# Four transformer layers on one core: image 1 loaded behind all weights, experts of image 0 with every fourth group of tangents, eight buffers for combined outputs

## The chip, the cores and the metric

The kernel runs on one core of a Trainium2 chip. The metric is the device time of one execution in microseconds (us). Its engines work side by side, each through its own list of instructions in order: PE (TensorE, matrix products and the transposes made with an identity matrix), DVE (VectorE), ACT (ScalarE), POOL (GpSimd) and SP (SyncE), which issues most of the DMAs. ACT issues some DMAs too, from the same list that holds its activations, and POOL issues the gathers and scatters. An instruction that has to wait holds up everything behind it on its engine. In the profile, "SPq" and "ACTq" are the DMA issues of SP and ACT.

## What is computed

Two images of 256 channels and 32x32 pixels (1024 tokens each, N) go through four layers. Cut to what matters:

```python
x = x + conv_attention(group_norm(x))        # layer 0: 4 heads of 64, every token of both images attends to all
x = linear_attention_block(x)                # layer 1: per image, 8 heads of 64, softmax attention, residual
t = tokens(x)
t = t + window_attention(layer_norm(t))      # layer 2: windows of 64
t = t + moe(layer_norm(t))                   # layer 2: 8 experts, top 2, 256 -> 1024 -> 256, gelu
# layer 3: additive attention, per image
q, k = u @ Wt, u @ Wx                        # u = layer_norm(t), 32 units
e = (tanh(q[:, None] + k[None] + bh) @ Wa)   # 1024 x 1024 x 32 tangents per image
t = t + softmax(e) @ u
t = t + moe3(layer_norm(t))                  # layer 3: 8 experts, top 2, 256 -> 512 -> 256, gelu
out = pixels(t)
```

Only the two chosen experts of each token are computed. The tokens are sorted by expert on the chip into blocks of 128 rows; a block is gathered, multiplied with its expert's weights, and scattered to a buffer in DRAM, from which each token's two results are read back and added with their router weights.

## The kernel before

**Front (layers 0 and 1).** `run` loads image 0 (`image(xT, 0)`, lines 1370 to 1375: per 128 channels one large DMA on SP and a small one on ACT, since the pixels are stored turned by 32). `front` (line 336) then loads Wk, Wq, Wv and the biases on SP, then image 1, then calls `project0` (line 504) for the projections of layer 0. The weights of layers 1 and 2 (`weights()`) and Wo come after it in the program. In `project0`, each image's group norm is taken (`group_norm` L583 and L584, `pool_stats` L599 to L604, `rsqrt` L131 to L138), then the image is normalised on DVE, 1024 columns per instruction (L545), and four chunks of 512 columns are multiplied on PE into k, q and v (L529, L565). DVE and ACT take them out of PSUM. A scheduler orders each engine's instructions by its own estimate of when they can run: it put image 1's statistics (L583) between image 0's `rsqrt` steps.

**Attention of layers 0 and 1 (`attention`, line 190).** One long list of steps: chunks of 512 queries for a pair of heads, each chunk of 32 steps (layer 0) or 8 (layer 1). A step is two score products (L215, L216) on PE, an exponential on ACT (L218), a running sum on DVE (L227) and the value products (L237) on PE. What belongs to the end of a chunk is put into later steps: `divide` (L251 to L264) two steps after the chunk's last, and the chunk's `finish` four steps after (L277). For every second chunk of layer 0, `finish` is `output0` (L367, L372): the product of the divided result `q` with Wo, added to the image.

**Experts (`experts`, line 1070).** Per block: gather the rows (POOL, L1098), fetch both weight matrices (SP, L1092 and L1104), transpose the rows (PE, L1110), first product (L1127), copy (DVE, L1132), transpose (L1138), gelu with bias (ACT, L1143: four instructions of 128 columns), second product (L1151), bias (DVE, L1157), scatter (POOL, L1158). The function yields after each part of 512 hidden columns, and its callers decide between what these steps are put. A block of layer 2 has two such parts, one of layer 3 has one. Layer 2 has 39 blocks for both images together, with two buffers for weights; layer 3 has 23 per image, with three.

**Combining (`combine`, line 1188).** For each tile of 128 tokens two DMAs read the tokens' two results into a tile `yt` (one on each of two given queues), and two DVE instructions (L1197) add them to `t`. `yt` has three buffers.

**From layer 2 to layer 3 in `run`.** After 49 steps of layer 2's experts, `prepare(0)` combines image 0's eight tiles (loads on SP and on ACT), takes the statistics, normalises (L131 to L186) and projects to the keys and queries of the additive attention (L1246, L1251, L1256). Expert steps go on from its ninth step. Then the additive attention runs over 128 groups of tangents (64 per image): DVE adds the query to the keys (L1280), ACT takes the tangents (L1290, 128x4096), PE sums them with the weights (L1299); every eight groups there is a softmax (ACT L1352) and its product with the values (PE L1312, L1320). In the first half, every second group is followed by an expert step of layer 2. Around the middle, the rest of layer 2 is finished and image 1 is prepared. Then image 0 is routed for layer 3, and its experts (`first`, `third(0)`) are stepped with every third group, until the tangents end. After the tangents, the routing of image 1 (`ready(1, 1)`) alternates with steps of `first`; what is left of `first` is drained; then image 1's 23 blocks run (`third(1)`), with one step of `end(0)` each. `end` (line 1533) combines a tile, and after every fourth tile transposes two halves (L1544), copies them on ACT to `y_f` (L1549, two buffers) and stores them (L1552, L1554, both SP). At the very end `end(1)` runs alone.

The expert activation gelu and the softmax's exponential are in different tables of ACT; tangents run with either.

Of the kernel before, what the change touches and what calls it, by code (L numbers as in the profile page):

```python
# [87 lines left out]
class Stack:  # L88
# [101 lines left out]
    def attention(self, chunks, pools):  # L190

        nc = self.nc
        p_t, p_o, p_r, sb = pools
        steps = [(c, j) for c in chunks for j in range(c["n"])]
        weights = {}
        inverses = sb.tile([P, CH], F32, name="inverses", bufs=1)
        nc.gpsimd.memset(inverses, 0.0)

        def score(n):
            c, j = steps[n]  # L210
            q, (ka, kb) = c["q"](), c["k"](j)
            ps = p_t.tile([P, 2, CH], F32, name="ps_t")
            for half in range(2):
                part = slice(64 * half, 64 * half + 64)
                nc.tensor.matmul(ps[part, 0, :], lhsT=ka[:, part], rhs=q[0:64, :], start=True, stop=True)  # L215
                nc.tensor.matmul(ps[part, 1, :], lhsT=kb[:, part], rhs=q[64:128, :], start=True, stop=True)  # L216
            e = sb.tile([P, 2, CH], F32, name="e", bufs=4)
            nc.scalar.activation(e, ps, AF.Exp)  # L218
            weights[n] = e
            if j == 0:  # L220
                c["sum"] = e
            elif j == 1:
                s = sb.tile([P, 2, CH], F32, name="sum", bufs=2)
                nc.vector.tensor_tensor(s, c["sum"], e, ALU.add)
                c["sum"] = s
            else:
                nc.vector.tensor_tensor(c["sum"], c["sum"], e, ALU.add)  # L227

        def accumulate(n):
            c, j = steps[n]  # L230
            if j == 0:
                c["po"] = p_o.tile([P, 2, CH], F32, name="ps_o")
            e = weights.pop(n)
            for r, v in enumerate(c["v"](j)):
                for half in range(2):
                    part = slice(64 * half, 64 * half + 64)
                    nc.tensor.matmul(  # L237
                        c["po"][64 * r : 64 * r + 64, half, :], lhsT=v[part, :], rhs=e[part, r, :],
                        start=(j == 0), stop=(j == c["n"] - 1),
                    )  # L240
            if j == c["n"] - 1:
                o = sb.tile([P, 2, CH], F32, name="o", bufs=2)
                nc.scalar.copy(o[:, 0, :], c["po"][:, 0, :])
                nc.vector.tensor_copy(o[:, 1, :], c["po"][:, 1, :])  # L244
                c["po"] = o

        def divide(c):

            ps = p_r.tile([P, CH], F32, name="ps_row")
            for r in range(2):  # L250
                nc.tensor.matmul(  # L251
                    ps[64 * r : 64 * r + 64, :], lhsT=self.ones[:, 0:64], rhs=c["sum"][:, r, :],
                    start=True, stop=True,
                )
            total = sb.tile([P, CH], F32, name="total", bufs=1)
            number = c["number"]
            nc.scalar.activation(total, ps, AF.Copy, accum_out=self.added[:, number : number + 1])
            o = c["po"]
            nc.vector.tensor_tensor(o[:, 0, :], o[:, 0, :], o[:, 1, :], ALU.add)
            den = sb.tile([P, CH], F32, name="den", bufs=2)  # L260
            to = c["o"]()
            for half in (slice(0, CH // 2), slice(CH // 2, CH)):
                nc.vector.reciprocal(den[:, half], total[:, half])  # L263
                nc.vector.tensor_tensor(to[:, half], o[:, 0, half], den[:, half], ALU.mult)  # L264
            nc.gpsimd.tensor_tensor(inverses, inverses, den, ALU.add)  # L265


        todo = {}
        later = lambda at, *fs: todo.setdefault(at, []).extend(fs)
        at = 0  # L270
        for i, c in enumerate(chunks):
            c["at"] = at
            at += c["n"]
            c["number"] = i

            later(at + 2, lambda c=c: divide(c))
            later(at + 4, c["finish"])  # L277
            for k, extras in c.get("extras", {}).items():
                later(c["at"] + k, *extras)
            if i + 1 < len(chunks):  # L280
                later(at - 4, chunks[i + 1]["prepare"])

        chunks[0]["prepare"]()
        scored = 0
        for n in range(at + 5):
            ahead = 2 if 0 < n < at and steps[n][1] == 0 else 1
            while scored < min(n + ahead + 1, at):
                score(scored)
                scored += 1
            if n < at:  # L290
                accumulate(n)
            for f in todo.pop(n, []):
                f()
        nc.vector.tensor_reduce(self.extremes[:, 1:2], inverses, AX.X, ALU.max)
# [38 lines left out]
    def front(self, xT, weights, tokens, done):  # L333
# [6 lines left out]
        with ExitStack() as ctx:  # L340
# [3 lines left out]
            wk, wq, wv = (self.load(w, n, "(c p) o -> p c o", p=P) for n in ("wk", "wq", "wv"))  # L344
            bk, bq = (self.load(w, n) for n in ("bk", "bq"))
            bv = self.load_row(w, "bv")
            self.image(xT, 1)
            q0 = big.tile([P, CC, T], F32, name="q")
            k0 = big.tile([P, 4, T], F32, name="k")
            v0 = big.tile([P, NT, 4, 64], F32, name="v")  # L350
            with ExitStack() as start:
# [1 line left out]
                    pool(start, "l0_xn"), pool(start, "l0_ps", bufs=4, space=PSUM), xT,  # L353
                    (wq, wk, wv, bq, bk, bv), (q0, k0, v0),
                )
            w_in, w_out, gn_w, gn_b, b_out = weights()
            wo, bo = self.load(w, "wo", "(c p) o -> p c o", p=P), self.load(w, "bo")

            pools = self.attention_pools(ctx)
            p_r = pools[2]  # L360
# [13 lines left out]
            def chunk0(t, o):  # L374
                def finish():
                    if o == CC - 1:
                        output0(t)
                    if (t, o) == (NCH - 1, CC - 1):
                        first.close()
                        tokens()  # L380
                        pools1.append(pool(ctx, "l1_late", side="right"))


                cols = slice(t * CH, (t + 1) * CH)
                return {
                    "prepare": lambda: None,
                    "n": 4 * NT,
                    "q": lambda: q0[:, o, cols],
                    "k": lambda j: [
                        k0[64 * r : 64 * r + 64, j // NT, (j % NT) * P : (j % NT + 1) * P] for r in range(2)  # L390
                    ],
                    "v": lambda j: [v0[:, j % NT, j // NT, :]] * 2,
                    "o": lambda: q0[:, o, cols],
                    "finish": finish,
                }

# [111 lines left out]
    def project0(self, pool, psum, xT, weights, to):  # L508
# [26 lines left out]
        for t in range(NCH):  # L535
            cols = slice(t * CH, (t + 1) * CH)
            if t % 2 == 0:
# [2 lines left out]
                    pool, psum, xT, b,  # L540
                    lambda ps, rows: nc.tensor.matmul(ps, lhsT=group, rhs=rows, start=True, stop=True),
                )
                for c in range(CC):
                    at = slice(b * N, (b + 1) * N)
                    nc.vector.tensor_scalar(  # L545
                        xn[:, c, at], xT[:, c, at], mean[:, c : c + 1], rs[:, c : c + 1], ALU.subtract, ALU.mult
                    )


            for o in range(CC):  # L550
# [634 lines left out]
                    fetch_second(b + ahead)  # L1185
            yield True

    def combine(self, sb, t, given, top, i, queues):

        nc = self.nc  # L1190
        n = top.shape[2]
        y = sb.tile([P, 2, C], F32, name="yt", bufs=3)
        for k in range(2):
            at = (k * n + i) * P
            queues[k].dma_start(out=y[:, k, :], in_=given[at : at + P, :])
# [181 lines left out]
    def run(self):  # L1377
        tc, nc, ins = self.tc, self.nc, self.ins
        PER = N // P
        with ExitStack() as ctx:  # L1380
# [137 lines left out]

                return mixture(1, wp, lambda _: rows[1][b], given[0][b], BLOCKS, lambda _: slots)

            def prepare(b, bank, *queues):

                for i in range(b * PER, (b + 1) * PER):
                    self.combine(sb, t[:, i], all_given[b * 2 * N : (b + 1) * 2 * N], top[0][b], i - b * PER, queues)
                    stats(2, i)
                    yield
                for g in range(2 * b, 2 * b + 2):
# [2 lines left out]
                    self.additive_project(aa, g, uT, bank)  # L1530
                    yield

            def end(b, bank):

                for i in range(PER):
                    self.combine(sb, t[:, b * PER + i], given[0][b], top[1][b], i, (nc.sync, nc.scalar))
                    yield
                    if i % 4 != 3:
                        continue
# [1 line left out]
                    for c in range(CC):  # L1541
                        ps = bank()
                        for k in range(4):
# [1 line left out]
                                ps[:, k * P : (k + 1) * P], t[:, b * PER + i - 3 + k, c * P : (c + 1) * P],  # L1545
                                self.ident,
                            )
                        y = sb.tile([P, CH], F32, name="y_f")
                        nc.scalar.copy(y, ps)  # L1549
                        to = self.out[b, c * P : (c + 1) * P, :]  # L1550
                        n = min(CH, N - SHIFT - at)
                        nc.sync.dma_start(out=to[:, at + SHIFT : at + SHIFT + n], in_=y[:, :n])  # L1552
                        if n < CH:
                            nc.sync.dma_start(out=to[:, : CH - n], in_=y[:, n:])  # L1554

            with ExitStack() as side:
# [10 lines left out]
                for k in range(2 * BLOCKS + 3):  # L1569
# [4 lines left out]
                        self.extreme(other.value[4][:, 0, 0:1])  # L1574
                        inv.close()
                    second.step()
                for k, _ in enumerate(prepare(0, bank, nc.sync, nc.scalar)):
                    if k >= PER:
                        second.step()

# [2 lines left out]
            with ExitStack() as ad:  # L1583
                half = PER * self.FOURS
                bank = banks["h"]
                then = Steps(prepare(1, bank, nc.sync, nc.sync))
                routed = Steps(ready(1, 0, bank))
                first = None
                for n in self.additive_attention(
# [14 lines left out]
                    elif routed.done:  # L1604
                        if first is None:
                            first = Steps(third(0, routed.value))
                        if n % 3 == 0:
                            first.step()
            with ExitStack() as side:
                bank = in_turn(enter(side, "side_ps2", space=PSUM), "m", 3)  # L1610
# [2 lines left out]
                    other.step()  # L1613
                    first.step()
                first.drain()
                ending = Steps(end(0, bank))
                for _ in third(1, other.value):
                    ending.step()
                ending.drain()
                drain(end(1, bank))  # L1620
            weights.close()


# [556 lines left out]
```

## Time and profile before

| | us |
|---|---|
| runs (median of 3; lowest to highest) | 2527.17; 2526.05 to 2531.06 |
| the profiled execution, its own time | 2528.73 |
| its span, first to last instruction | 2527.0 |
| PE busy in the span | 2358.8 (93%) |
| DVE busy | 1703.0 (67%) |
| ACT busy | 1440.2 (57%) |
| start until the first attention score | 0 to 68.7 |
| attention of layers 0 and 1 | 68.7 to about 1330 |
| window attention and layer 2's experts alone | about 1330 to 1720 |
| combining and preparing image 0 | 1721 to 1760 |
| tangents | 1760 to 2331 |
| routing of image 1 | 2336 to 2392 |
| experts of image 1 | 2392 to 2500 |
| last combination and output | 2500 to 2527 |

Busy shares are averages over stages with different limits, so each stage has to be read by itself: a table of busy time by stretch shows which engine is full there, and the list of waits shows what the fullest engine waits for. A line of the timeline holds the start, the duration from the first start to the last end of the merged instructions, the engine, the line, and in square brackets the idle time before it with what ended it.

### The profile page before, as it was taken

The page shows a single profiled execution, that of the slowest core. Times are in us where ns is not written, and L with a number is a line of the kernel's source. Part 1 is how long each engine was busy: PE and PEld are TensorE (multiplying, and loading weights), DVE is VectorE, ACT ScalarE, POOL GpSimd, SP SyncE. Part 2 cuts the span into 40 slices and gives each one's busy share as a digit, 9 for nine tenths or more (in the row PEclk, how much of TensorE's full clock was granted, in tenths as well). Part 3 has the DMA queues.
Part 4 walks back from the last instruction along what each step waited for, and adds up shares of the span by engine and source line. Part 5 has one row for each costly group of instructions (what it writes and reads, how often), then busy time and mean ns, then how long its engine had stood idle before and what let it go on. Part 6 is the DMA issues. An engine that isn't in the chain of part 4 may idle for free.

```text
span 2527.0 us, 42429 instructions
## 1 busy us (share of the span) xinstructions
PE 2358.8 (93%) x17211; PEld 1029.1 (41%) x17211; DVE 1703.0 (67%) x2612; ACT 1440.2 (57%) x1628; POOL 240.3 (10%) x254
## 2 busy tenths in 40 slices
PE   6999999999999999999998979998999888999896
PEld 3333333333333333333333646664444333344564
DVE  4677777775677777866678566226777787786533
ACT  1565556645565566544453433222999998999221
POOL 0000000000000000000001312221110001121241
PEclk9999999999999999999999979999999999999898
DMA  4000000000000000000000037875333202233796
GB/s 133 5 1 1 1 1 2 1 1 1 1 1 1 1 2 1 1 1 1 1 1 10 2 118 265 302 284 194 138 137 136 75 9 78 86 119 115 244 337 204
DMA packets 58929, 190.51 MB, mean 75 GB/s; under 512 B 14116, under 2 KB 28964, under 8 KB 48740
## 3 DMA queue, kind: packets, MB, share of 16 engines
q1 hardware_dynamic: 45812, 161.93, 18.5%
q0 software_dynamic: 8160, 22.29, 2.4%
q10 hardware_dynamic: 4752, 3.48, 0.5%
q8 instruction: 137, 2.24, 0.4%
q14 instruction: 68, 0.56, 0.1%
HBM read 168.15 MB, written 17.43 MB: 73 GB/s over the span
## 4 chain that ended last, share of the span: by engine, by line
PE 73%; DVE 11%; issue 7%; ACT 4%; DMA 3%; POOL 1%; ACTq 0%; SPq 0%; DVEq 0%; POOLq 0%
PE ps_o L237 20%; PE ps_t L215 19%; PE ps_e L1299 8%; PE bk_h L1127 5%; PE bk_y L1151 4%; PE ps_pt L1320 2%; PE ps_row L445 2%; DVE sum L227 2%; DVE th L1280 2%; DMA w<-in_l_w 2%; ACT th L1290 1%; DVE den L263 1%; PE ps_qk L529 1%; PE ps_row L431 1%; PE bk_t L1138 1%
## 5 line engine op out<-in xcount | busy, mean ns | idle before, releaser
L227 DVE TENSOR_TENSOR sum<-sum,e 128x1024 f32<-128x1024 f32 x592 | 725.1, 1225 | 311.0 <-ACT e L218 300.9
L218 ACT ACTIVATE e<-ps_t 128x1024 f32<-128x1024 f32 x640 | 653.9, 1025 | 466.8 <-PE ps_t L216 463.5
L237 PE MATMUL ps_o<-e,v 64*64 64x512 f32 x5120 | 675.0, 591 | 8.3 <-DVE o L244 7.7
L215 PE MATMUL ps_t<-q,k 64*64 64x512 f32 x2048 | 532.3, 591 | 0.5 <-DVE v L569 0.5
L216 PE MATMUL ps_t<-q,k 64*64 64x512 f32 x2048 | 532.3, 591 | 0.0
L1280 DVE TENSOR_SCALAR th<-kT,qb 128x1024 f32<-128x1024 f32 x478 | 331.3, 750 | 95.1 <-PE ps_e L1299 92.9
L237 PEld LDWEIGHTS ps_o<-e,v 64*64 64x64 f32 x5120 | 193.8, 132 | 369.3 <-issue 178.3
L1290 ACT ACTIVATE th<-th 128x4096 f32<-128x4096 f32 x94 | 336.5, 3646 | 6.0 <-DVE th L1280 5.9
L1143 ACT ACTIVATE h<-bk_t,w 128x128 f32<-128x128 f32 x496 | 142.3, 375 | 270.4 <-issue 159.4
L1299 PE MATMUL ps_e<-th,pick 128*32 128x512 f32 x2048 | 271.8, 620 | 23.9 <-ACT p L1352 9.3
L215 PEld LDWEIGHTS ps_t<-q,k 64*64 64x64 f32 x2048 | 149.1, 133 | 287.1 <-issue 152.9
L1127 PE MATMUL bk_h<-w,xgT 128*128 128x512 f32 x496 | 245.7, 611 | 12.8 <-DVE xgT L1115 7.9
L1151 PE MATMUL bk_y<-w,h 128*128 128x256 f32 x992 | 248.3, 386 | 6.2 <-DVE y L1157 3.4
L1151 PEld LDWEIGHTS bk_y<-w,h 128*128 128x128 f32 x992 | 178.5, 192 | 56.7 <-issue 27.4
L1132 DVE COPY hp<-bk_h 128x512 f32<-128x512 f32 x124 | 85.4, 689 | 131.6 <-PE bk_h L1127 130.1
L265 POOL TENSOR_TENSOR inverses<-inverses,den 128x512 f32<-128x512 f32 x24 | 30.5, 1269 | 1333.5 <-DVE den L263 1333.5
L216 PEld LDWEIGHTS ps_t<-q,k 64*64 64x64 f32 x2048 | 149.1, 133 | 0.0
L215 PE MATMUL ps_t<-qh,kh 64*64 64x512 f32 x512 | 138.2, 597 | 0.0
L216 PE MATMUL ps_t<-qh,kh 64*64 64x512 f32 x512 | 137.3, 596 | 0.0
L1299 PEld LDWEIGHTS ps_e<-th,pick 128*32 128x32 f32 x2048 | 58.8, 111 | 170.8 <-issue 116.3
L1158 POOL DMA_INDIRECT given<-y,gives x85 | 86.9, 1022 | 415.7 <-DVE y L1157 365.2
L1127 PEld LDWEIGHTS bk_h<-w,xgT 128*128 128x128 f32 x496 | 87.4, 194 | 85.1 <-issue 56.5
(334 smaller groups left out, 2063.7 us busy)
## 6 DMA issues: line engine op xcount, KB each, us to landing
w<-in_l_w SPq DMA_DIRECT2D x39, 1152.0 KB
w<-in_l_w SPq DMA_DIRECT2D x39, 1030.0 KB
w<-in_l_w SPq DMA_DIRECT2D x46, 640.0 KB
w<-in_l_w SPq DMA_DIRECT2D x46, 514.0 KB
yt<-given SPq DMA_DIRECT2D x40, 128.0 KB
rows<-u SPq DMA_DIRECT2D x8, 512.0 KB
yt<-given ACTq DMA_DIRECT2D x24, 128.0 KB
k<-k SPq DMA_DIRECT2D x16, 128.0 KB
```

The costliest lines, as they stand in the source:

```text
L215: nc.tensor.matmul(ps[part, 0, :], lhsT=ka[:, part], rhs=q[0:64, :], start=True, stop=True)
L216: nc.tensor.matmul(ps[part, 1, :], lhsT=kb[:, part], rhs=q[64:128, :], start=True, stop=True)
L218: nc.scalar.activation(e, ps, AF.Exp)
L227: nc.vector.tensor_tensor(c["sum"], c["sum"], e, ALU.add)
L237: nc.tensor.matmul(c["po"][64 * r : 64 * r + 64, half, :], lhsT=v[part, :], rhs=e[part, r, :], start=(j == 0), stop=(j == c["n"] - 1),)
L1127: nc.tensor.matmul(ps, lhsT=inputs[b][:, c, :], rhs=first[b][:, at : at + CH], start=(c == 0), stop=(c == CC - 1),)
L1143: nc.scalar.activation(hidden[b, n][:, cols], ps[:, cols], AF.Gelu, bias=first[b][:, at : at + 1])
L1151: nc.tensor.matmul(sums[b], lhsT=h[:, j * P : (j + 1) * P], rhs=second[b][:, at : at + C], start=(n == 0 and j == 0), stop=(n == HH - 1 an ...
L1158: nc.gpsimd.indirect_dma_start(out=given[b], out_offset=index(slots(b)[1], b), in_=y, in_offset=None)
L1280: nc.vector.tensor_scalar(h[:, j, :], *keys_and_queries(n, j), None, ALU.add)
L1290: nc.scalar.activation(h, h, AF.Tanh)
L1299: nc.tensor.matmul(scored[i][U * j : U * (j + 1), a, :], lhsT=aa["pick"][:, m, :], rhs=h[:, j, a * CH : (a + 1) * CH], start=(m == 0), sto ...
```

## The change

Seven edits, in five places.

1. In `front`, all weights (of layers 1 and 2, and Wo) are loaded before image 1, which now comes last on SP's list.
2. In `project0`, the normalisation is made in pieces of 512 columns, both channel halves of the first piece ahead of the second.
3. A chunk can set its own lag; the chunks of layer 0 set it to 6, so `output0` comes six steps after the chunk's last, not four.
4. `combine` takes its pool and the number of its buffers. `prepare(0)` and both calls of `end` use a pool of their own with eight `yt` buffers; `prepare(1)` keeps three.
5. `first`, the experts of layer 3 for image 0, is stepped with every fourth group of tangents, not every third.
6. `y_f` gets four buffers, from the new pool.
7. The small second store of an output (32 columns) is issued by ACT, not by SP.

```diff
-            later(at + 4, c["finish"])
+            later(at + c.get("lag", 4), c["finish"])
...
             bv = self.load_row(w, "bv")
+            w_in, w_out, gn_w, gn_b, b_out = weights()
+            wo, bo = self.load(w, "wo", "(c p) o -> p c o", p=P), self.load(w, "bo")
             self.image(xT, 1)
...
-            w_in, w_out, gn_w, gn_b, b_out = weights()
-            wo, bo = self.load(w, "wo", "(c p) o -> p c o", p=P), self.load(w, "bo")
...
                     "o": lambda: q0[:, o, cols],
+                    "lag": 6,
                     "finish": finish,
...
-                for c in range(CC):
-                    at = slice(b * N, (b + 1) * N)
-                    nc.vector.tensor_scalar(
-                        xn[:, c, at], xT[:, c, at], mean[:, c : c + 1], rs[:, c : c + 1], ALU.subtract, ALU.mult
-                    )
+                for at in range(b * N, (b + 1) * N, CH):
+                    for c in range(CC):
+                        nc.vector.tensor_scalar(
+                            xn[:, c, at : at + CH], xT[:, c, at : at + CH],
+                            mean[:, c : c + 1], rs[:, c : c + 1], ALU.subtract, ALU.mult,
+                        )
...
-    def combine(self, sb, t, given, top, i, queues):
+    def combine(self, sb, t, given, top, i, queues, bufs=3):
...
-        y = sb.tile([P, 2, C], F32, name="yt", bufs=3)
+        y = sb.tile([P, 2, C], F32, name="yt", bufs=bufs)
...
-            def prepare(b, bank, *queues):
+            def prepare(b, bank, of, bufs, *queues):
...
-            def end(b, bank):
+            def end(b, bank, of):
...
-                    self.combine(sb, t[:, b * PER + i], given[0][b], top[1][b], i, (nc.sync, nc.scalar))
+                    self.combine(of, t[:, b * PER + i], given[0][b], top[1][b], i, (nc.sync, nc.scalar), PER)
...
-                        y = sb.tile([P, CH], F32, name="y_f")
+                        y = of.tile([P, CH], F32, name="y_f", bufs=4)
...
-                            nc.sync.dma_start(out=to[:, : CH - n], in_=y[:, n:])
+                            nc.scalar.dma_start(out=to[:, : CH - n], in_=y[:, n:])
...
-                for k, _ in enumerate(prepare(0, bank, nc.sync, nc.scalar)):
+                for k, _ in enumerate(prepare(0, bank, enter(side, "outputs2"), PER, nc.sync, nc.scalar)):
...
-                then = Steps(prepare(1, bank, nc.sync, nc.sync))
+                then = Steps(prepare(1, bank, sb, 3, nc.sync, nc.sync))
...
-                        if n % 3 == 0:
+                        if n % 4 == 0:
                             first.step()
...
-                ending = Steps(end(0, bank))
+                of = enter(side, "outputs3")
+                ending = Steps(end(0, bank, of))
...
-                drain(end(1, bank))
+                drain(end(1, bank, of))
```

More of the change, by code (lines that the diff above doesn't have):

```diff
@@ L1519, in third @@
                 return mixture(1, wp, lambda _: rows[1][b], given[0][b], BLOCKS, lambda _: slots)
-            def prepare(b, bank, *queues):
+            def prepare(b, bank, of, bufs, *queues):
                 for i in range(b * PER, (b + 1) * PER):
-                    self.combine(sb, t[:, i], all_given[b * 2 * N : (b + 1) * 2 * N], top[0][b], i - b * PER, queues)
+                    self.combine(of, t[:, i], all_given[b * 2 * N : (b + 1) * 2 * N], top[0][b], i - b * PER, queues, bufs)
                     stats(2, i)
```

## The prediction

> **What bounds the kernel now.** The page's busy shares (PE 93%) hide the stages, so the first view is busy time by stretch, with the mean clock granted to PE, the share of DMA and GB/s behind it:
>
> ```profile
> core 0: us, PE busy (x) PEld busy (x) DVE busy (x) ACT busy (x) POOL busy (x), PEclk, DMA share, GB/s
> ...
> 18.00:69.00 51.00, 45.70 (x136) 25.98 (x138) 23.02 (x52) 5.47 (x8) 0.00 (x0) 0.97 0.27 68
> 1720.00:1760.00 40.00, 31.95 (x109) 18.98 (x108) 29.18 (x94) 7.01 (x23) 4.16 (x4) 0.87 0.60 205
> ...
> 1795.00:1980.00 185.00, 181.86 (x1096) 87.77 (x1097) 144.88 (x242) 181.30 (x141) 16.42 (x15) 1.00 0.38 132
> ...
> 2155.00:2335.00 180.00, 166.57 (x1018) 75.02 (x1020) 136.54 (x239) 177.29 (x122) 29.90 (x26) 0.96 0.32 108
> 2335.00:2384.00 49.00, 44.89 (x226) 30.00 (x218) 32.26 (x116) 16.26 (x42) 11.74 (x12) 1.00 0.70 234
> 2384.00:2400.00 16.00, 7.86 (x21) 4.11 (x22) 5.08 (x15) 0.36 (x2) 6.69 (x7) 0.58 0.74 265
> ```
>
> While tangents run (1760 to 2331) ACT is full: 98% of both long stretches. PE is as full in the first half (181.86 of 185) and has room in the second (166.57 of 180). After them PE leads (44.89 of 49), then stands half idle in 2384 to 2400, the gap between the routing of image 1 and its experts. The chain of waits leads through the same places. Next, the waits of PE within the attention of layers 0 and 1:
>
> ```profile
> PE ps_row L367 <- DVE q L264: 5.1, 4, 1.3
> ```
>
> Four `output0` products of layer 0 wait 5.1 us together. Then the timeline of the ends; first the start, where image 0's normalisation (L545) waits:
>
> ```profile
> 12.28 0.70 DVE L583 BATCH_NORM_STATS2 gn_st<-xT 128x6 f32<-128x512 f32 x1 [2.02 <-DMA xT<-in_x]
> ...
> 16.42 1.54 DVE L545 TENSOR_SCALAR xn<-xT,gs,rs 128x1024 f32<-128x1024 f32 x2
> 17.29 0.50 PEld L529 LDWEIGHTS ps_qk<-xn,sb_wk 128*128 128x128 f32 x2 [7.79 <-DVE xn L545]
> ```
>
> DVE stands idle for image 1, whose statistics are in its list in the middle of image 0's `rsqrt`. Then `prepare(0)`, ACT's list:
>
> ```profile
> 1729.03 3.98 ACTq L1195 DMA_DIRECT2D yt<-given  x3
> 1736.37 1.15 ACT L1143 ACTIVATE h<-bk_t,w 128x128 f32<-128x128 f32 x4 [8.81 <-DMA yt<-given]
> ...
> 1759.88 3.62 ACT L1290 ACTIVATE th<-th 128x4096 f32<-128x4096 f32 x1 [1.01 <-DVE th L1280]
> ```
>
> ACT's gelu stands behind loads that wait for one of three `yt` buffers; PE, which needs the gelu, idles about 8 us in 1720 to 1742. Last, the gap at 2391 and the end:
>
> ```profile
> 2391.62 0.66 PE L1110 MATMUL bk_x<-ident,xg 128*128 128x128 f32 x2 [8.03 <-DMA xg<-rows,takes]
> ...
> 2393.28 3.62 PE L1127 MATMUL bk_h<-w,xgT 128*128 128x512 f32 x4
> ...
> 2502.92 7.52 ACTq L1195 DMA_DIRECT2D yt<-given  x7
> ...
> 2516.06 1.01 DVE L1197 SCALAR_TENSOR_TENSOR t<-yt,top,t 128x256 f32<-128x256 f32 x2 [1.94 <-DMA yt<-given]
> ```
>
> PE waits 8 us for gathered rows and then runs at half clock (3.62 where the same four take 1.88 elsewhere); at the end, loads are issued only as `yt` buffers come free.
>
> **What the Trainium skill says.** "DMA: Bandwidth & Descriptors", section "Issuing engines are not separate DMA queues": transfers of SP, ACT and POOL run on the same 16 engines, and a second issuer saves only the issuing time. So eight buffers let loads start, but don't widen the path; before shows both issuers held 7.5 us by buffers, not by width (125 GB/s in 2500 to 2527). "ScalarE: Activation LUTs", "What ACT_TABLE_LOAD costs": 1283 ns and a drain of some 1380 ns for every switch; the trace has 1.28 us, and its next activation starts 1.29 after, so I count no drain. "TensorE: Matmul & The Clock Gate", "What's actually happening": half clock after an idle window of about 3.4 us; 0.58 in 2384 to 2400 agrees.
>
> **The change part by part.** The sum is against the profiled execution's own 2528.73 (span 2527.0), 1.56 above the median of 2527.17.
>
> *Start.* Image 1's four statistics (4 x 0.69) and the wait leave the way: in the changed kernel's lists they come after the first v products. `rsqrt` then runs through: image 0 started it (L131) at 9.82, and for the second image L131 at 42.19 leads to L545 at 44.63, 2.44. So L545 starts at 12.26. A piece of 512 columns: 0.81 at 1024, and 0.41 at 256 in the same form (L160), so some 0.54. Products then start 0.06 later (0.87 less 0.81): 12.86 against 17.29, -4.4. For the second image the piece saves 0.27 again. PE is full between (45.70 of 51), so both reach the end: **-4.7**. Image 1 now lands behind about 6.5 MB; at some 290 to 390 GB/s that is 17 to 23 us, and DVE needs it at about 26 (the t=0 products take PE until then). If later, DVE stalls and part returns: bounds -5 and +1.
>
> *Lag.* The four `output0` go two steps back, behind score products that PE can do; two steps are longer than the 1.3 of the longest wait. Each `norm` that follows keeps about 2 us. **-5.1**, bounds -3.5 (some of it returns as waits at later products) and -5.5.
>
> *prepare(0).* All 16 loads go out together; DVE's combination (10.2 us from 1723.87) runs without pauses, and ACT is free for gelu. But SP's weight fetches now stand behind eight loads, and DVE does the whole combination ahead of the experts' copies. In the lists, 51 gelu halves stand before the first tangents, not 53. I take the normalised tokens at PE at 1738.1 instead of 1741.2, and first tangents at about 1756.9: -3.0; but two halves more (2 x 1.0 of ACT) fall into the ACT-bound tangents: +2.0. **-1.0**, bounds +5 (weights late behind the loads) and -5 (the 8 us of idle PE all filled).
>
> *Every fourth group.* Up to the last softmax ACT has 89 gelu halves, not 93, and two table loads fewer. One is 1.01 as ACT spends it: -(4 x 1.01 + 2 x 1.28) = -6.6, all in the second half, where ACT has no room and PE does. What remains of `first` grows from 8 blocks to 12. A layer 3 block is 1.72 + 0.44 + 1.73 + 0.22 = 4.1 on PE. By the lists ten of twelve run before the routing's last product, two after. So two more come beside the routing, +8.2, of which the idle there (49 - 44.89 = 4.1) can be filled and PE's lag at the last tangents (5.05) shrinks, about -5 of it in all (taken as 5.2): +3.0. Two more fall into the 8.03 wait for rows; two down products stand in PE's list behind the first gathered rows, +3.5, against a warm clock at 2393 (3.62 - 1.88): +1.8, which I take as paid for by the shorter wait ahead of it. So +3.0 for the stage, and **-3.6** in all. Bounds: +4 (nothing fills) and -9 (all fills).
>
> *Experts of image 1.* 23 blocks of 4.62 us each, DMA and PE both over 90%: not touched, **0**. The first blocks' weights were late before, since SP's `yt` loads stand ahead of them (11.59 us at 2387.94, the fetch at 2400.8). With eight buffers they don't wait for a buffer, but they do wait for the scatter of the last block of `first`, which is now later. A wait replaces a wait; ±3.
>
> *Tail.* With eight buffers the 16 loads (2.1 MB) are issued in some 3 us and land at the 300 GB/s of the stretch before: about 7 us, until 2511, in place of about 2515.5. DVE adds at 0.4 to 0.5 each, done at about 2512.6 instead of 2517.1: -4.5. Transposes and copies follow as before. A store on ACT instead of SP frees the last issues (1.54 and 0.87 behind each other): -0.5. **-5.0**, bounds -2 (loads land no faster) and -6.5.
>
> Sum: -4.7 - 5.1 - 1.0 - 3.6 + 0 - 5.0 = -19.4, so 2509.3 for an execution like the profiled, and less 1.56 **2508** on the median.
>
> **The rivals.**
> *PE binds the first half.* There PE is as full as ACT (181.86 against 181.30 of 185). Halves moved from before the tangents cost PE more than ACT's 1.0 (a half is about 4 us of PE), so 2 x 4 instead of 2 x 1: +6, and filling beside the routing fails by 2: 2516. For it: those numbers; against: 24 us of the middle (1980 to 2155) in which PE idles and could take it.
>
> *The gap is filled entirely.* The wait of 8.03 and the cold clock vanish, the weights of image 1's blocks come early, and `prepare(0)` wins its whole 5: -4 -6 more, 2498. For it: 16 us at half use in 2384 to 2400. Against: rows need the routing's result, whatever PE does.
>
> *The loads don't do what is said.* Image 1 lands after 26, or the `yt` loads are limited by the transfers themselves: half of start and tail is lost, +4.5: 2512.
>
> *Slower.* One mechanism: the late last scatter of `first`. Its four more blocks come out exposed (4 x 4.1 = 16.4), because ACT, now bound by loads of `end(0)` that wait for that scatter (6.9 from scatter to load in before: 2381.06 to 2387.94), can't do the gelu of image 1's first block behind them, and SP can't fetch its weights (4.6 in the chain of before): 16.4 + 6.9 + 4.6 = 27.9. With no gain on ACT in the tangents, the rest gives -15.8: +12.1, 2539. It decides once the stretch from the last tangent to image 1's fourth block grows by more than the 22.4 that the other parts (-15.8 and ACT's -6.6) give. For it: both queues wait ahead of needed work. Against: image 1's rows come no sooner than the scatter.
>
> **How the numbers follow.** A measurement of this kernel tells 0.2% (5 us) from no change. The forecast (2508) 0.63; PE-bound 2516, 0.14; filled 2498, 0.12; loads 2512, 0.05; slower 2539, 0.06, of which 0.01 is within 0.2%. In the first four the time stays below 2522, except 0.02 at their upper end. So faster 0.92, same 0.03, slower 0.05. The range 2498 to 2518 is the forecast's own: the bounds of the parts, +5 and -4 at prepare(0), +7 and -5 at the experts, ±3 at the weights, don't all fall on one side; by their squares they make about ±10. It also takes in the two nearest rivals.
>
> **What would show it right or wrong.** L545 starts near 12.3 and PE at 12.9, with no wait of DVE on `xT` after 20. No wait of `ps_row` L367 on `q`. The first tangents near 1747 (1759.88 less 4.7, 5.1 and 3.0). The stretch from first to last tangent some 4.6 shorter. From last tangent to the first row product of image 1's experts some 3 longer, and its first block warm. From the last scatter to the end, 5 shorter. It is wrong if the stretch after the tangents grows by over 10, if ACT stands before a `yt` load with a gelu behind it near 2390 to 2400, or if the tangents' stretch isn't shorter.

## The result, and the profile after

The changed kernel takes 2513.16 us (median of 4, 2511.86 to 2515.10) beside 2529.11 for the kernel before (4 runs): a ratio of 0.9943, 95% interval 0.9927 to 0.9959. That is 10 to 18 us faster; 19 were forecast.

Lines of the changed kernel stand one or two further down: L545 is L546, L1143 is L1145, L1195 and L1197 are L1197 and L1199, L1290 is L1292. Busy time by stretch, changed kernel, with the same columns as before:

```profile
core 0: us, PE busy (x) PEld busy (x) DVE busy (x) ACT busy (x) POOL busy (x), PEclk, DMA share, GB/s
...
1710.00:1750.00 40.00, 27.91 (x99) 16.82 (x98) 28.81 (x94) 6.10 (x15) 3.74 (x4) 0.83 0.50 173
1785.00:1970.00 185.00, 182.15 (x1096) 87.62 (x1095) 144.56 (x242) 181.21 (x141) 17.11 (x16) 1.00 0.39 132
2145.00:2320.00 175.00, 157.19 (x977) 67.09 (x970) 131.95 (x233) 172.35 (x111) 26.41 (x23) 0.96 0.25 88
2320.00:2380.00 60.00, 56.58 (x268) 38.22 (x267) 36.23 (x128) 17.19 (x50) 20.20 (x22) 1.00 0.84 286
2380.00:2400.00 20.00, 16.68 (x64) 11.34 (x63) 8.39 (x18) 4.61 (x14) 6.38 (x7) 0.83 0.90 303
```

The tangents are as full on ACT as they were; behind them PE is now 94% busy through the routing. What is left of the gap lies in 2380 to 2400, at a clock of 0.83. The timeline of the start and of the end:

```profile
12.78 3.78 PE L530 MATMUL ps_qk<-xn,sb_wk 128*128 128x512 f32 x4 [3.28 <-DVE xn L546]
...
26.11 1.27 DVE L585 BATCH_NORM_STATS2 gn_st<-xT 128x6 f32<-128x512 f32 x2
```
```profile
2492.96 5.93 SPq L1197 DMA_DIRECT2D yt<-given  x8
2493.04 6.13 ACTq L1197 DMA_DIRECT2D yt<-given  x8
...
2497.82 5.49 DVE L1199 SCALAR_TENSOR_TENSOR t<-yt,top,t 128x256 f32<-128x256 f32 x13 [0.70 <-DMA yt<-given]
```

The first product starts 4.5 earlier (17.29 before), and image 1's statistics find it there at 26.11, with no wait on the DMA. At the end all sixteen loads are out within some 6 us (3 were forecast) and DVE adds thirteen times with hardly a pause. That is most of the story; the rest needs each stage by itself. From the timelines I took where each stage begins and ends: first score, last score, first expert transpose, first `yt` load of `prepare(0)`, first and last tangent, first product of image 1's experts (L1127 of before), that of its fourth block, their last product, the last scatter, the end.

| stage, us | forecast | before | changed | difference |
|---|---|---|---|---|
| to the first score | -4.7 | 68.65 | 64.12 | -4.53 |
| attention | -5.1 | 1287.41 | 1284.32 | -3.09 |
| to the first expert transpose | 0 | 148.02 | 147.76 | -0.26 |
| layer 2's experts alone | 0 | 217.03 | 218.75 | +1.72 |
| first yt load to first tangents | -3.0 | 38.76 | 33.66 | -5.10 |
| tangents | -4.6 | 570.70 | 563.67 | -7.03 |
| to image 1's first expert product | +3.0 | 62.71 | 65.68 | +2.97 |
| from there to block 4 | 0 | 12.17 | 15.97 | +3.80 |
| from block 4 to the last scatter | 0 | 95.88 | 97.52 | +1.64 |
| last scatter to end | -5.0 | 25.68 | 19.65 | -6.03 |
| sum (span) | -19.4 | 2527.01 | 2511.10 | -15.91 |

One profile of each is not enough for the small ones. Twelve more runs follow below, most of which leave most stages alone: over all fourteen profiles layer 2's experts took 214.1 to 219.5, and the stretch from block 4 to the last product 94.2 to 98.6. So a single pair with +1.72 or +1.64 is no evidence; on the second, averages say a little more (see `ends_only`). A profile is also one execution, and can lie up to 7.5 from the median of its kernel. The other stages repeat within 3 where the kernels do the same in them, the tangents within some 6.

### The profile page after: what moved, and what is told of

It is laid out like the page before. It is cut to its first block, busy times and chain, and to the rows that moved or that the text cites. A ratio compares the mean times of both kernels' runs of the same rounds, so it can differ in the third digit from the quotient of the medians.

```text
span 2511.1 us, 42409 instructions
## 1 busy us (share of the span) xinstructions
PE 2357.0 (94%) x17211; PEld 1029.9 (41%) x17211; DVE 1700.8 (68%) x2616; ACT 1435.9 (57%) x1626; POOL 241.3 (10%) x254
## 4 chain that ended last, share of the span: by engine, by line
PE 70%; DVE 10%; ACT 8%; issue 7%; DMA 4%; POOL 1%; ACTq 0%; SPq 0%; DVEq 0%; POOLq 0%
PE ps_o L237 20%; PE ps_t L215 19%; PE ps_e L1301 6%; PE bk_h L1129 4%; PE bk_y L1153 4%; ACT th L1292 3%; DVE sum L227 2%; PE ps_row L446 2%; DMA w<-in_l_w 2%; PE ps_pt L1322 2%; PE ps_qk L530 1%; PE ps_row L432 1%; DVE den L263 1%; DVE th L1282 1%; PE ps_row L457 1%
## 5 line engine op out<-in xcount | busy, mean ns | idle before, releaser
L227 DVE TENSOR_TENSOR sum<-sum,e 128x1024 f32<-128x1024 f32 x592 | 725.1, 1225 | 303.7 <-ACT e L218 292.8
L218 ACT ACTIVATE e<-ps_t 128x1024 f32<-128x1024 f32 x640 | 652.8, 1024 | 464.7 <-PE ps_t L216 463.2
L1292 ACT ACTIVATE th<-th 128x4096 f32<-128x4096 f32 x94 | 335.7, 3649 | 5.6 <-DVE th L1282 5.6
L1145 ACT ACTIVATE h<-bk_t,w 128x128 f32<-128x128 f32 x496 | 142.2, 374 | 269.2 <-issue 158.3
```

The source lines that it names most:

```text
L1145: nc.scalar.activation(hidden[b, n][:, cols], ps[:, cols], AF.Gelu, bias=first[b][:, at : at + 1])
L1292: nc.scalar.activation(h, h, AF.Tanh)
```

## The experiments

**One part at a time.** Four kernels, each the kernel before with one part.

```diff
-            later(at + 4, c["finish"])
+            later(at + c.get("lag", 4), c["finish"])
...
-            for b, at, first_step, apart in ((0, NCH, 8, 4), (1, NCH * CC + 5, N // P - 2, 1)):
+            for b, at, first_step, apart in ((0, NCH, 10, 4), (1, NCH * CC + 5, N // P - 2, 1)):
```

`lag_only` has the first pair, with a lag of 6 for layer 0; the second pair is in `lag_norm10` alone, beside the lag. `start_only` has edits 1 and 2 of the change; `n4_only` edit 5.

> The kernel before with the lag of 6 alone. As predicted: the four waits of ps_row L367 go, 5.1 us, and nothing takes their place, so the attention of layers 0 and 1 ends 5.1 earlier. Rival, from the trace of the changed kernel: the statistics of image 0's norm come late by the same two steps, its second small product (ps_gs) waits about 1.1 and PE then runs at half clock for some us more, so 2 to 3 us of 6 come back and 3.1 stay.

> The kernel before with the lag of 6 and image 0's norm at step 10 of its chunk instead of 8. If the return is the norm's wait two steps after the later output0 (rival of the run above), it is as short again as before and the attention ends 5 to 6 earlier than before, 2.3 more than with the lag alone. If the return has another cause, the attention ends as with the lag alone, about 3.1 earlier.

> The kernel before with the order of the loads and the normalisation in pieces alone. As predicted: first product at 12.8 and everything after 4.5 to 4.7 earlier up to the end, -4.6 on the time. Rival: a part comes back where image 1's statistics stand after t=0's v products, or later in a stage that transfers bind; then less than 3 at the end.

> The kernel before with every fourth group alone. As predicted: the tangents 6.6 shorter, the stage from the last tangent to image 1's experts 3.0 longer, the experts themselves as before, -3.6 at the end. Rival, from the trace of the changed kernel: the last scatter of image 0's experts now lands after image 1's first block is ready for its gelu, ACT stands before a load of end(0) for 3 to 5 us with that gelu behind it, and the kernel is at best 1 us faster, or slower by up to 3.

| kernel | ratio to before, interval | what its stage shows |
|---|---|---|
| lag_only | 0.9979 (0.9965 to 0.9994) | attention 1284.23 |
| lag_norm10 | 0.9985 (0.9975 to 0.9995) | attention 1280.33, then 151.95 to the first expert transpose |
| start_only | 0.9993 (0.9982 to 1.0004) | first score at 63.10 |
| n4_only | 1.0002 (0.9991 to 1.0013) | tangents 561.37, to first product 65.37, to block 4 15.29 |

*The lag.* The distance between ACT's exponentials (L218) tells where the attention gains and loses; each of layer 0's eight chunks has 64 steps with one each (not 32, as the description above has it). With the lag the three earlier `output0` gain 1.50, 1.56 and 1.56, and the fourth 0.74: 5.36 in all, where 5.1 was forecast. But from the ninth to the seventeenth exponential of the fifth chunk, where image 0's norm stands, the time is 23.44 with the lag and 20.91 before. The timeline there (changed kernel) and the same wait in `before`, then PE's clock in three-microsecond stretches (`lag_only`, and `before` below it; the columns are those of the table by stretch):

```profile
532.86 2.50 DVE L227 TENSOR_TENSOR sum<-sum,e 128x1024 f32<-128x1024 f32 x2
532.89 1.05 PE L410 MATMUL ps_gs<-gn_mv,whole 128*128 128x1 f32 x8
...
536.07 1.60 PE L410 MATMUL ps_gs<-gs_d,whole 128*128 128x1 f32 x8 [1.13 <-DVE gs_d L606]
```
```profile
PE ps_gs L409 <- DVE gs_d L604: 0.2, 1, 0.2
```
```profile
538.00:541.00 3.00, 1.98 (x12) 1.08 (x12) 2.79 (x6) 0.22 (x1) 0.00 (x0) 1.00 0.00 0
541.00:544.00 3.00, 2.89 (x16) 2.25 (x20) 0.95 (x7) 0.00 (x0) 0.00 (x0) 0.54 0.02 5
544.00:547.00 3.00, 3.00 (x16) 0.90 (x12) 1.26 (x2) 1.02 (x1) 0.00 (x0) 0.50 0.00 0
547.00:550.00 3.00, 3.00 (x26) 1.07 (x22) 2.76 (x11) 1.07 (x2) 0.00 (x0) 0.83 0.00 0
```
```profile
541.00:544.00 3.00, 2.79 (x21) 1.82 (x24) 1.75 (x6) 0.00 (x0) 0.00 (x0) 0.98 0.02 5
544.00:547.00 3.00, 3.00 (x16) 0.96 (x12) 1.20 (x7) 1.02 (x1) 0.00 (x0) 0.50 0.00 0
547.00:550.00 3.00, 3.00 (x30) 1.23 (x26) 2.75 (x10) 1.04 (x2) 0.00 (x0) 0.95 0.00 0
```

PE's second small product waits 1.13 for DVE: the last `output0` came two steps later, so the statistics did too, and two running sums that they had held up (L227, 2.50) stand ahead of the step that PE needs. Before, the wait was 0.21. PE then runs at half clock ("cold") for 6.8 us, where before it was 3.4. With the norm at step 10 the wait is 0.36 and the same stretch took 19.36 at full clock. So what came back is the norm's wait and the cold clock behind it, as the rival said. Yet the timed ratio is no better. The trace says where the 3.9 went: right after the attention, PE waits for DVE in both kernels. `lag_only` first, `lag_norm10` second:

```profile
1354.00:1358.00 4.00, 1.33 (x12) 0.21 (x8) 3.69 (x4) 1.06 (x2) 0.00 (x0) 1.00 0.00 0
1358.00:1362.00 4.00, 3.71 (x11) 1.47 (x12) 3.27 (x5) 0.69 (x2) 0.00 (x0) 1.00 0.00 0
```
```profile
1350.00:1354.00 4.00, 1.32 (x10) 0.44 (x12) 3.79 (x4) 0.58 (x1) 0.00 (x0) 0.82 0.00 0
1354.00:1358.00 4.00, 4.00 (x7) 1.19 (x5) 2.38 (x3) 0.69 (x2) 0.00 (x0) 0.50 0.00 0
1358.00:1362.00 4.00, 4.00 (x9) 1.71 (x8) 4.00 (x5) 0.00 (x0) 1.26 (x1) 0.83 0.00 0
```

PE is busy 1.3 of 4 in both; in one the clock stays at 1.00, in the other it halves.

*The start* gains at the first score what was forecast (-5.6 in this profile). The timed gain, 0.0018 at most, is 4.6 at most; its middle is 1.8. Where the rest of it would go is not shown: the profiled execution was the fastest of its 14 (2519.41, the median is 2526.88), so its stages cannot tell.

*The fourth group* gains 9.3 in the tangents of this profile and gives back 5.8 up to block 4; in time it is nothing, where -3.6 was forecast.

**The rest alone, and two ways to mend the fourth group.** `after_again` is the changed kernel once more, `ends_only` the kernel before with edits 4 (in `end`), 6 and 7, `prepare_only` with edit 4 in `prepare(0)`. The edits within `start_only` and within `ends_only` were not parted further. `after_n3` is the changed kernel with every third group, and `after_end0_late`:

```diff
-                for _ in third(1, other.value):
-                    ending.step()
+                for k, _ in enumerate(third(1, other.value)):
+                    if k > 3:
+                        ending.step()
```

> The changed kernel once more, as the measure for the next two on the same chip: 0.994 of before, 14 to 15 us, in both theories. From the last tangent to image 1's first product some 3 longer than before, and from there to its last product some 3 to 5 longer, with PE waiting 3.3 for the gelu (ACT h) that stands behind a load of end(0).

> The changed kernel with every third group again. As predicted: 3.6 slower than the changed kernel (tangents 6.6 longer, the stage after them 3.0 shorter). Rival (the gain of the fourth group is given back at image 1's first blocks by the load of end(0) ahead of the gelu): the wait of PE on ACT h is gone, image 1's experts 3 to 4 shorter, and the time within 1 us of the changed kernel's.

> The changed kernel, with the first step of end(0) four expert steps later, so that ACT and SP have the gelu and the weights of image 1's first blocks ahead of the loads that wait for the last scatter. Rival: the wait of PE on ACT h (3.3) and the cold stretch behind it go, image 1's experts are 3 to 5 shorter, and the kernel is 3 to 5 faster than the changed one, 17 to 20 faster than before. As predicted (the experts of image 1 bound by DMA and PE, the loads not in the way): no change against the changed kernel, within 1 us.

> The kernel before with eight yt buffers in both calls of end, four y_f buffers and the small store on ACT alone. As predicted: from the last scatter to the end 5.0 shorter, image 1's experts as before, -5.0 in all. Rival: end(0)'s sixteen loads, going out at once, hold up image 1's weights and take 2 to 3 of it back.

> The kernel before with eight yt buffers in prepare(0) alone. As predicted: from the first yt load to the first tangents 3.0 shorter, and the tangents 2.0 longer for the two expert halves that now fall among them; -1.0 in all. Rival, from the traces of the changed kernel: the first stretch is 5 to 6 shorter, the tangents 2 to 3 longer, about -3.5 in all.

| kernel | ratio to before, interval | tangents | to first product | to block 4 | last scatter to end |
|---|---|---|---|---|---|
| after_again | 0.9939 (0.9921 to 0.9956) | 562.63 | 66.97 | 15.38 | 20.59 |
| after_n3 | 0.9917 (0.9895 to 0.9939) | 572.27 | 63.05 | 11.18 | 20.42 |
| after_end0_late | 0.9925 (0.9905 to 0.9945) | 563.12 | 65.62 | 13.91 | 20.82 |
| ends_only | 0.9977 (0.9966 to 0.9987) | 569.65 | 62.60 | 11.63 | 22.04 |
| prepare_only | 0.9986 (0.9978 to 0.9995) | 568.49 | 62.57 | 12.26 | 25.22 |

`ends_only` gains 5.8 (0.0023), with 3.6 of it in the tail of this profile. Its eight buffers do not slow image 1's first blocks (11.63), but its rival, that the loads of `end(0)` hold up image 1's weights, is not ruled out: from block 4 to the last scatter this profile took 100.2, against 95.9 before. Over the eight profiles with eight buffers in `end` that stretch took 98.7 on average, over the six others 97.0; the ranges overlap (97.5 to 100.3, 95.9 to 98.6), and the cause is not shown.

`after_n3` was forecast 3.6 slower than the changed kernel; its median is 5.3 lower than that of `after_again`, with overlapping intervals, and its first blocks are short again (11.18), as the rival said.

`prepare_only` gains 3.5 in time (0.0014). In it the first tangents come 33.44 after the first load (38.76 before), and the tangents are not longer than in other kernels with every third group (566.6 to 572.8). The timeline of the changed kernel shows how:

```profile
1715.03 3.72 ACTq L1197 DMA_DIRECT2D yt<-given  x6
...
1722.89 1.12 PE L1140 MATMUL bk_t<-ident,hp 128*128 128x128 f32 x4 [7.45 <-ACT h L1145]
...
1732.22 1.91 PE L182 MATMUL bk_m<-ident,u 128*128 128x128 f32 x8
...
1748.60 3.62 ACT L1292 ACTIVATE th<-th 128x4096 f32<-128x4096 f32 x1 [1.16 <-DVE th L1282]
```

SP's eight loads and ACT's first six are out within 7 us. DVE's combination now runs ahead of the experts' copies and ends 12.5 after the first load (18.9 before). So the eight transposes of the first half of the tokens run in one piece, 17.3 after the first load (20.7 before, in two pieces with two of an expert's products between them). The tangents follow 16.4 behind, not 18. But ACT is not free for gelu, as was forecast: its loads stand ahead of the gelu together, and PE waits 7.45 for it. In the eight profiles with eight buffers in `prepare(0)` this wait is 3.7 to 7.5, in the six others 2.4 at most. So the stage is shorter though PE idles more than before: the steps that lead to the first tangents come from DVE.

The blocked gelu is in the timeline of ACT and PE, changed kernel:

```profile
2382.27 1.88 PE L1129 MATMUL bk_h<-w,xgT 128*128 128x512 f32 x4
2385.64 0.36 ACTq L1197 DMA_DIRECT2D yt<-given  x1
2386.12 0.37 ACT L1145 ACTIVATE h<-bk_t,w 128x128 f32<-128x128 f32 x1 [13.26 <-DMA xg<-rows,takes]
...
2387.47 1.12 PE L1140 MATMUL bk_t<-ident,hp 128*128 128x128 f32 x4 [3.31 <-ACT h L1145]
2388.37 3.62 PE L1153 MATMUL bk_y<-w,h 128*128 128x256 f32 x8
```

The wait that the profile puts down to `xg` had long ended: the block's rows were turned at 2373 to 2375. What ACT stood before is the load on the line above it, which reads what the last scatter (issued at 2379.66) wrote. The gelu could have started at 2382.2, when its transposes (L1140) were done; it started at 2386.12. PE waits 3.31 and then makes its products at half clock (3.62 for eight; 1.89 at full clock in `sp_late6`). Beginning `end(0)` four steps later left the first load where it was in ACT's list, ahead of that gelu, because the scheduler orders the list by its own estimate: the wait shrank to 2.1 and the stretch to 13.91 only, so this run does not decide it. The next two put both loads of `end(0)` on SP and begin it seven steps later (`sp_late6`), also with every third group (`sp_late6_n3`):

```diff
-                    self.combine(of, t[:, b * PER + i], given[0][b], top[1][b], i, (nc.sync, nc.scalar), PER)
+                    self.combine(of, t[:, b * PER + i], given[0][b], top[1][b], i, (nc.sync, nc.scalar if b else nc.sync), PER)
...
+                    if k > 6:
```

> The changed kernel with both loads of end(0) on SP and end(0) begun seven expert steps later, so that no load stands ahead of a gelu on ACT, and the first weights stand ahead of the loads on SP. If the load ahead of the gelu is what lengthens image 1's first blocks: no wait of PE on ACT h, from its first product to that of its fourth block about 12.2 as before (15.5 in the changed kernel), and 3 to 4 faster than the changed kernel. If it is the weights or the transfers: the stretch stays above 14.

> The same with every third group. Where the load ahead of the gelu is the only cost of the fourth group at the experts, this one is slower than the run with the fourth group by what is left of its gain: tangents 8 to 9 longer, the stretch after them 3.4 shorter, so 4.5 to 5.5. If the fourth group is worth nothing in any case, the two are within 2.

Waits of PE in the experts of image 1 (us in total, times, longest), changed kernel (from 2370), then `sp_late6` (from 2370), and below them the stretch from image 1's first product to that of block 4, in the same order:

```profile
PE bk_h L1129 <- DMA w<-in_l_w: 5.7, 5, 1.9
PE bk_t L1140 <- ACT h L1145: 3.3, 1, 3.3
PE bk_x L1112 <- DMA xg<-rows,takes: 1.6, 1, 1.6
...
```
```profile
PE bk_h L1129 <- DMA w<-in_l_w: 6.6, 5, 3.6
PE bk_x L1112 <- DMA xg<-rows,takes: 2.1, 1, 2.1
...
```

```profile
2377.96:2393.92 15.96, 12.64 (x45) 8.46 (x44) 7.66 (x17) 2.95 (x11) 4.92 (x6) 0.79 0.87 311
```
```profile
2375.21:2387.82 12.61, 9.02 (x41) 5.52 (x39) 4.69 (x10) 3.42 (x12) 5.87 (x7) 1.00 0.75 273
```

`sp_late6`: to block 4 12.60, no wait on `h`; median 2508.19, ratio 0.9932 (0.9912 to 0.9951). `sp_late6_n3`: 2513.76, 0.9947 (0.9930 to 0.9964), tangents 569.67 against 561.69, to the first product 62.48 against 66.07. So with no load ahead of the gelu the first blocks are as short as before. The wait itself was exchanged, not removed: PE now stands 3.6 for the weights of block 4. What is shorter is PE's busy time, 9.02 instead of 12.64, because the half clock does not fall into this stretch, nor do products of `end(0)`; a part of that only moves behind block 4. The whole stage, from the first product to the last scatter, tells what stays: 110.2 in `sp_late6`, against 113.5 and 114.2 in the two profiles of the changed kernel and 109.9 on average in the eight with every third group. This run moves the loads to SP and the start of `end(0)` together; the later start alone, with a load still ahead of the gelu (`after_end0_late`), left the stage at 114.2. With both, the fourth group is worth 8.0 less 3.6 less 1.1 (11.54 against 12.60 to block 4), 3.3 in the profiles and 5.6 between the medians, whose intervals overlap.

**Both together.** `both_mended` is `sp_late6` with the norm at step 10.

> The run with both loads of end(0) on SP and a later start of end(0), and image 0's norm at step 10 beside it. If the stretch behind the norm is ruled by its wait and by the cold clock that follows, the attention ends 4 earlier than in that run (1280.3 instead of 1284.2), and the time is 0.9915 to 0.9925 of before, unless the idle stretch between attention and layer 2 then happens to fall to half clock as it did with the norm at step 10 before (4.3 longer up to the experts); in that case the time is that run's. If the attention is not shorter, the reading of the return is wrong. Image 1's first to fourth block again near 12.6.

Attention 1280.35, then 151.78 to the first expert transpose: the gain comes and goes as in `lag_norm10`. To block 4 11.88. Median 2510.64, ratio 0.9923 (0.9909 to 0.9936). `sp_late6` and `both_mended` are the best versions of the study by their profiles (spans 2505.3 and 2506.9), but no interval parts them from the changed kernel, nor from `after_n3`.

## Why the prediction came out as it did

The side and the range were right; the gain was some 4 us too large. That it was no more than 4 is in part luck: `prepare(0)` gained 4.0 more than forecast, the lag 2.9 less, and image 1's first blocks lost 3.4 that were put at nothing. Means over all profiles that share a part tell the steps apart.

- *Start*, -4.7 forecast: 63.67 over eight kernels against 68.73 over six, -5.1. Right at its place; image 1 was there in time.
- *Lag*, -5.1 forecast: the waits went as forecast (5.36), but the attention gained 2.2 (1284.17 over seven, against 1286.39 over five). The step that failed is "Each `norm` that follows keeps about 2 us": image 0's waited 0.9 more than before, and with the longer half clock behind it lost 2.5. (The rest of the difference is that two of the five kernels with the old lag were at full clock there with no edit that touches it.) The lower bound of -3.5 was too tight because it priced a wait by its length and not by the clock after it.
- *prepare(0)*, -1.0 forecast: half the mechanism was right. DVE's combination ran without long pauses ahead of the experts' copies; but ACT did not become free for gelu, and PE's idle time was not filled. The term of the first stretch was too small: it measured -5.8 (33.97 over eight, 39.74 over six), against -3.0; the two halves moved into the tangents cost 0.8 at every third group (570.1 over three, 569.3 over five; within the spread), against 2.0. Transposes in one piece came with tangents closer behind them, which I had priced at nothing.
- *Every fourth group*, -6.6 in the tangents and +3.0 behind: 563.5 over five against 570.1 over three, -6.6; to the first product 65.9 over six against 62.5 over eight, +3.4. Both right, and for the reason given: between first and last tangent ACT has 40 gelu halves and 22 table loads in the changed kernel, 44 and 24 in `after_n3`.
- *Experts of image 1*, 0 forecast with ±3: the first blocks lost 3.4 (15.55 over the three profiles with the fourth group, a load on ACT and `end(0)` from the first step, against 12.15 over the eight with every third). The sentence "A wait replaces a wait" failed: 1.3 for the weights became 3.3 for the gelu, with the half clock behind it. One sign that the prediction itself named for being wrong came true, ACT before a `yt` load with a gelu behind it (at 2385.6). The rival on the slower side had the mechanism, ACT bound by a load of `end(0)` with the gelu behind it; the argument held against it, that "image 1's rows come no sooner than the scatter", was wrong: the rows were turned from 2373 on, the last scatter was issued at 2379.66, and the load behind it went out at 2385.6. Its price was 3 to 4, not 27.9: the four more blocks cost only the 3.4 above, and PE hardly waited for weights before block 4 (0 and 1.0 in the two profiles of the changed kernel).
- *Tail*, -5.0: 20.59 over eight against 25.58 over six, -5.0.

The sum of the measured steps is -5.1 -2.2 -5.0 -6.6 +3.4 +3.4 -5.0 = -17.1, and the timed ratios of the changed kernel (0.9943, 0.9939) make -14.4 and -15.4 of 2529, with -17.1 inside their intervals. With the 1.7 by which the kernels with eight buffers in `end` were longer behind block 4, the sum is -15.4. The five parts timed alone give 5.3, 1.8, -0.5, 5.8 and 3.5, together 15.9, each with an interval of some 2 to 4 to either side.

In the Trainium skill's "TensorE: Matmul & The Clock Gate", section "What's actually happening", the clock is set from a window of about 3.4 us that runs freely and does not start anew with the kernel. That agrees with what the traces show here: the half clock behind the norm lasted 0, 3.4 or 6.8 us. The eight exponentials behind the norm took 20.9 us in three kernels with the lag of 4 and 19.2 in two others whose work there is the same, and the clock was 0.50 in the first three and 1.00 in the two. With the lag, its longer wait and the norm at step 8 it was cold for 6.8 us seven times of seven (23.3 to 23.4). Why the clock in the 16 us after the attention was 0.79 both times with the norm at step 10, and 1.00 in all twelve other profiles, stays open: a window that runs freely would hardly choose so.

## What to carry to other kernels

A DMA issue on ACT that reads what a scatter writes binds every activation behind it, so where work is moved later, look for the issues that wait for its last write and at what stands behind them in the same list. A wait's price on PE is its length plus the half clock that may follow, here 2.5 us where the wait itself grew by 0.9; a gain of a microsecond or two from a shift can go or double by that alone. An engine that a change was to free should be looked at afterwards: here the stage got shorter by 5.8 while PE's wait for ACT grew. And a stage that no edit touches should be measured over several kernels before a difference in it is explained.

## What was not expected of the hardware

The same work at the same place ran at full or half clock from one kernel to the next (19.21 and 20.91 for the eight exponentials behind the norm). In `before` the 3.4 us at half clock follow a wait of PE of only 0.21, among sixteen products of 128x1. Layer 2's experts, with DMA busy for 0.7 to 0.8 of their time, varied by 5.4 us (214.1 to 219.5) between kernels that do the same there, and runs of the kernel before spread over 2519.6 to 2539.9, so that a gain of some 2 us (`start_only`) could not be told from none with 14 runs.
